# Fetching the last tile of some groups row by row from SyncE's queue in a two-layer graph network

## The chip, the cores and the metric

The kernel runs on one core of a Trainium2 chip. A core has TensorE (PE) for matrix products, VectorE (DVE), ScalarE (ACT), GpSimd (POOL) and SyncE (SP), each with its own queue of instructions, and 16 DMA engines[...]. The metric is device time in microseconds (us), the median of several runs; lower is better.

## The reference

12500 nodes with 64 features, 212500 edges sorted by target node. Each layer gathers a row for the source of every edge, makes a message of it and adds the message to the row of the edge's target. Cut to what matters:

```python
h = jnp.maximum(_layernorm(x, axis=-1), 0.0)
# layer one: 16 relations, each with a 64x64 weight
msg = jnp.zeros(...)
for r in range(16):
    mask = etypes == r
    msg = msg + h[src] * mask[:, None] @ weight[r]
x = x + segment_sum(msg, dst, num_segments=12500)

h = jnp.maximum(_layernorm(x, axis=-1), 0.0)
# layer two
z = relu(concatenate([h[src], h[dst], edge_attr], axis=1) @ W1 + b1)
x = x + segment_sum(z @ W2 + b2, dst, num_segments=12500)
```

All data are float32.

## The kernel before

Edges are taken in order of their targets, 128 at a time: a tile. Four tiles make a group (`G = 4`); there are 1661 tiles with edges (`NTR`) and 416 groups (`NGR`, the last holds one tile). A check in front sends the inputs of this case to `in_order`, which runs `first_layer` and then `second_layer`, each a loop over groups with a few steps lagging behind the group that is being loaded.

**Gathers.** `gather` (line 414) allocates a buffer `rows` of 128 x 4 x 64 values, one of 14, and issues one indirect DMA on GpSimd's queue for every tile of the group (line 419): 128 rows of 256 bytes, from `h_rows` in layer one (the normalised nodes) or from `a_rows` in layer two (the source's part of the first product, W1's upper block applied to the normalised nodes). The row numbers lie in `src_i`, one column per tile. These are GpSimd's only instructions in the two layers.

**Layer one.** For a group, ScalarE makes a one-hot table of relation and target (`relations`, `off_r` and `oh_r`). Two groups later (`L1_PE`) TensorE multiplies each tile's rows with it (`products`, line 577, two matrix products per tile, into `pa`), and five groups later (`L1_ADD`) VectorE adds `pa` into a table of the current nodes. When a block of 256 nodes is complete, `finish` (line 488), spread over the following iterations, applies the relation weights, normalises, and stores `a_rows` and `b_rows` from SyncE's queue. SyncE also loads `part` and `step` (lines 371 to 375) and turns the edge attributes into bfloat16 parts (`attributes`: `attr_a` in, `attr_p` out).

**Layer two.** Per group, SyncE loads `bw` (40 rows of `b_rows` at an address from a register, line 689) and `at9` (the attributes, line 693; `at` in the profile), each with ten buffers, and every fourth group `local_bc` (line 681, three buffers, 480 KB). Every eighth group `windows` (line 436) loads eight addresses into SyncE's registers. ScalarE makes the one-hot `ohT`, TensorE puts target part and attribute part into `pz`. Three groups later (`L2_Z`) VectorE adds the gathered rows: `z = pz + rows` (line 717). Then come the relu (`hid`), the product with a one-hot of the target (`pa`), and the addition into `sums` nine groups later.

**Order.** `V_`, `S_`, `T_` and `Q_` (line 474) keep the instructions of VectorE, ScalarE, TensorE and SyncE in the order in which the program writes them; `Q_` is SyncE. GpSimd's gathers go straight to its queue. A few loads that use `nc.sync` directly may be moved by the scheduler. Buffers are reused when their last reader is done; a DMA of SyncE's queue also waits on the semaphore that the DMA eight places before it used. Layer two's gathers wait until all of `a_rows` is written.

Of the kernel before, what the change touches and what calls it, by code (L numbers as in the profile page):

```python
# [30 lines left out]
F32 = mybir.dt.float32  # L34
BF16 = mybir.dt.bfloat16
I32 = mybir.dt.int32
AF = mybir.ActivationFunctionType
ALU = mybir.AluOpType
# [5 lines left out]
P = 128  # L44
N = 12500
# [29 lines left out]

L1_PE, L1_ADD = (2, 1), (5, 2)
L2_Z, L2_HID, L2_PE, L2_ADD = (3, 1), (4, 1), (6, 1), (9, 1)


def turns(lag):  # L80

    most, least = lag
    of = {}
    for g in range(NGR):
        of.setdefault(g + max(least, min(most, most - (g - (NGR - 40)) // 4)), []).append(g)
    return of
# [40 lines left out]
def gnn_kernel(  # L127
# [161 lines left out]
    def in_order():  # L289
        with ExitStack() as c2:  # L290
# [120 lines left out]
                V_.tensor_scalar(code, d, -1.0, 1.0, op0=ALU.mult, op1=ALU.add)  # L411
                yield

            def gather(table, idx, g):
                t = wk.tile([P, G, D], F32, name="rows", bufs=14)
                tiles = [i for i in range(G) if g * G + i < NTR]
                for i in tiles:
                    k = g * G + i
                    G_.indirect_dma_start(  # L419
                        out=t[:, i, :],  # L420
                        out_offset=None,
                        in_=table,
                        in_offset=bass.IndirectOffsetOnAxis(ap=idx[:, k : k + 1], axis=0),
                    )
                return t, len(tiles)

            def relations(code, k, n):

# [31 lines left out]
            class InOrder:  # L460


                def __init__(self, engine):
                    self.engine = engine
# [102 lines left out]
            def first_layer(psA):  # L567
                local_targets()
                for _ in codes(0, *load_part(0)):
                    pass  # L570
                clear(tables[1][:, :, AHEAD:])
                open_step, beside, coming = iter(()), iter(()), iter(())
                n_of, oh_of, rows_of, pa_of = {}, {}, {}, {}
                of_pe, of_add = turns(L1_PE), turns(L1_ADD)
                chunk = 0

                def products(g, i):
                    for half in range(2):
                        T_.matmul(
                            pa_of[g][half * D : (half + 1) * D, i, :],  # L580
                            lhsT=rows_of[g][:, i, :],
                            rhs=oh_of[g][:, i, half * HW : (half + 1) * HW],
                            start=True,
                            stop=True,
                        )

                def add(a, i):
                    k = a * G + i
                    if i < n_of[a]:
                        ca, ka = divmod(k, NT // NCH)  # L590
                        if k % RG == 0:
                            at.update(enumerate(windows(codes_of[ca][1], ka, SN + AHEAD - WT, V_), k))
                        to = tables[STEP[a] % 2][:, :, bass.ds(at.pop(k), WT)]
                        V_.tensor_tensor(to, to, pa_of[a][:, i, :].rearrange("p (r n) -> p r n", r=RH), op=ALU.add)

                at = {}
                for it in range(NGR + L1_ADD[1]):
                    g = it
                    if g < NGR:
                        c, gc = divmod(g, NGR // NCH)  # L600
                        if gc == NGR // NCH // 4 and c + 1 < NCH:
                            part = load_part(c + 1)
                        if gc == NGR // NCH // 2 and c + 1 < NCH:
                            coming = codes(c + 1, *part)
                        if g % 12 == 6 and chunk < EP // (P // EA) // ACH:
                            for _ in beside:
                                pass
                            beside = attributes(chunk)
                            chunk += 1
                        rows_of[g], n_of[g] = gather(h_rows[:, :], src_i, g)  # L610
                        if n_of[g]:
                            oh_of[g] = relations(codes_of[c][0], gc * G, n_of[g])
                    now, adds = of_pe.get(it, []), of_add.get(it, [])
                    for g in now:
                        if n_of[g]:

                            pa_of[g] = psA.tile([P, G, HW], F32, name="pa", bufs=5)
                    for j in range(max(len(now), len(adds))):
                        for i in range(G):
                            if j < len(now) and i < n_of[now[j]]:  # L620
                                products(now[j], i)
                            if j >= len(adds):
                                continue
                            a = adds[j]
                            add(a, i)
                            for _ in range(1 if a <= FIN[NREG - 1] else 2 if a <= FIN[NFIN - 2] else 3):
                                next(open_step, None)
                            next(coming, None)
                            if i % 2:
                                next(beside, None)  # L630
                        if j < len(adds) and adds[j] in FIN:
                            k = FIN.index(adds[j])
                            for _ in open_step:
                                pass
                            if k + 1 < NFIN:
                                go_on(k)
                            open_step = finish(k, psA)
                for _ in beside:
                    pass
                for _ in open_step:  # L640
                    pass
# [23 lines left out]
            def second_layer(ps):  # L665
# [3 lines left out]
                open_step = iter(())  # L669
                a_of, n_of, oh_of, pz_of, hid_of, pa_of = {}, {}, {}, {}, {}, {}  # L670
                at, at_b = {}, {}
                of_z, of_hid, of_pe, of_add = turns(L2_Z), turns(L2_HID), turns(L2_PE), turns(L2_ADD)
                for it in range(NGR + L2_ADD[1]):

                    g = it
                    if g < NGR:
                        if g % RG == 0:
                            at_b.update(enumerate(windows(first_row, g, PAD_DST, Q_), g))
                        if g % RB == 0:
# [2 lines left out]
                                local_bc,  # L682
                                dst_l[g : g + RB, :].rearrange("g e -> (g e)").unsqueeze(0).to_broadcast([W3, RB * G * P]),
                            )
                        a_of[g], n_of[g] = gather(a_rows[:, :], src_i, g)
                        n = n_of[g]
                        if n:
                            bw = wk.tile([W3, D], BF16, name="bw", bufs=10)
                            Q_.dma_start(
                                bw, b_rows[bass.ds(at_b.pop(g), W), :].rearrange("n (k d) -> k n d", k=3)  # L690
                            )
                            at9 = wk.tile([A9, G * P], BF16, name="at9", bufs=10)
                            Q_.dma_start(
                                at9,
                                attr_p[:, :, g * G * P : (g + 1) * G * P]
                                .rearrange("k i e -> (k i) e")
                                .unsqueeze(0)
                                .to_broadcast([3, 3 * EA, G * P]),
                            )
                            off = wk.tile([W3, G * P], BF16, name="off")  # L700
                            ohT = wk.tile([W3, G * P], BF16, name="ohT", bufs=6)
                            S_.activation(
                                off, local_bc[:, (g % RB) * G * P : (g % RB + 1) * G * P], AF.Abs, bias=neg_w
                            )
                            S_.activation(ohT, off, AF.Relu, bias=1.0, scale=-1.0)
                            if g % 2 == 0:
                                pz = ps.tile([P, 2, G, D], F32, name="pz", bufs=4)
                            pz_of[g] = pz[:, g % 2]
                            for i in range(n):
                                cols = slice(i * P, (i + 1) * P)  # L710
                                T_.matmul(pz_of[g][:, i, :], lhsT=ohT[:, cols], rhs=bw, start=True, stop=False)
                                T_.matmul(pz_of[g][:, i, :], lhsT=at9[:, cols], rhs=w1c_9, start=False, stop=True)
                    for g in of_z.get(it, []):
                        n = n_of[g]
                        if n:
                            hid_of[g] = wk.tile([P, G, D], F32, name="z", bufs=3)
                            V_.tensor_tensor(hid_of[g][:, :n, :], pz_of.pop(g)[:, :n, :], a_of.pop(g)[:, :n, :], op=ALU.add)
                    for g in of_hid.get(it, []):
                        n = n_of[g]
                        if n:  # L720
# [493 lines left out]
```

## Time and profile before

| | us |
|---|---|
| median of three runs (5110.07 to 5111.33) | 5110.31 |
| the profiled execution, its own time | 4236.6 |
| its span, from the first to the last instruction | 4234.8 |
| first gather of layer one starts at | 45.27 |
| first gather of layer two starts at | 2152.24 |

The profiled execution is shorter than the runs that make up the median. All that the profile says is about that one execution. Its TensorE clock was granted in full (1.000).

Some of the stages, as busy time per engine (us from the span's start; the last columns are the share of the 16 DMA engines in use and what they moved):

| stage | length | PE | DVE | ACT | POOL | DMA share | GB/s |
|---|---|---|---|---|---|---|---|
| 1000 to 1500 (layer one) | 500 | 327.1 | 142.2 | 279.2 | 379.0 | 0.20 | 43 |
| 2700 to 3500 (layer two) | 800 | 261.3 | 135.1 | 268.0 | 604.7 | 0.32 | 71 |

How to read the lines further below. A group of instructions is given by source line (L469 is the line of the helper that keeps the order, so many groups share it), engine, operation, what it writes and reads, and its count; then busy time, mean nanoseconds of one, and the idle time of its engine just before, with what ended it. In a list of waits a line is: engine and tile that waited, for what, us in total, times, longest. In a timeline it is: start, duration, instruction, and in brackets the idle time before it. In the answer for one tile, a line is: instruction and count, shortest, median and longest duration in ns, and its first and last start in us. SPq is SyncE's queue; its DMA lines give the issue and not the transfer.

### The profile page before, as it was taken

How to read it: one execution, taken by the hardware profiler on the slowest of the kernel's cores; microseconds unless marked ns; L12 is line 12 of the kernel's file. 1: busy time of each engine (PE TensorE's matmuls, PEld its weight loads, DVE VectorE, ACT ScalarE, POOL GpSimd, SP SyncE). 2: the span in 40 equal slices, each digit the busy share in tenths (PEclk: the TensorE clock that was granted, in tenths of full speed). 3: DMA queues.
4: the chain of work that ended last, by engine and by line, in shares of the span. 5: the costliest groups of instructions: out<-in, count | busy, mean ns of one | idle time of the engine just before them, and what ended most of it. 6: DMA issues, size and time to landing. Idle time of an engine off the chain costs nothing.

```text
span 4234.8 us, 51468 instructions
## 1 busy us (share of the span) xinstructions
PE 2048.8 (48%) x15300; PEld 1509.6 (36%) x15300; DVE 971.8 (23%) x4076; ACT 1884.2 (44%) x3872; POOL 3158.4 (75%) x3342
## 2 busy tenths in 40 slices
PE   1666666666666666666643333333333333333333
PEld 1444434344444444444432222222222223222223
DVE  4222222223222222222211111111111111111111
ACT  6555555555455555554533333333333333333323
POOL 4777777777777777777767777777777777777776
DMA  5212221212122211111133333333333333333332
GB/s 130 43 39 44 43 44 42 44 40 47 39 44 42 44 39 34 32 31 31 32 77 69 74 70 70 73 71 70 69 74 71 69 74 70 70 73 71 70 67 47
DMA packets 289856, 241.32 MB, mean 57 GB/s; under 512 B 177127, under 2 KB 220143, under 8 KB 289463
## 3 DMA queue, kind: packets, MB, share of 16 engines
q0 software_dynamic: 106816, 110.79, 14.5%
q1 hardware_dynamic: 167241, 123.53, 11.0%
q10 hardware_dynamic: 15510, 3.61, 0.4%
q8 instruction: 124, 2.03, 0.2%
q14 instruction: 165, 1.35, 0.1%
HBM read 212.57 MB, written 25.10 MB: 56 GB/s over the span
## 4 chain that ended last, share of the span: by engine, by line
POOL 44%; DMA 29%; issue 23%; PE 5%; ACT 0%; POOLq 0%; DVE 0%; DVEq 0%; ACTq 0%
POOL rows L419 43%; DMA rows<-h_rows,src_i 15%; DMA rows<-a_rows,src_i 13%; PE pT L469 3%; PE pa L469 2%; DMA first_row<-in_first 1%; POOLq L419 0%; PE pab L469 0%; ACT table L469 0%; DVE sums L469 0%; DVE z L469 0%; ACT hid L469 0%; DMA a_rows<-ab 0%; ACT off_r L469 0%; POOLq L1210 0%
## 5 line engine op out<-in xcount | busy, mean ns | idle before, releaser
L419 POOL DMA_INDIRECT rows<-h_rows,src_i x1661 | 1584.7, 954 | 542.1 <-issue 418.8
L419 POOL DMA_INDIRECT rows<-a_rows,src_i x1661 | 1567.2, 944 | 522.3 <-issue 457.7
L469 PE MATMUL pa<-oh_r,rows 128*64 128x96 f32 x6644 | 932.1, 391 | 747.3 <-DMA rows<-h_rows,src_i 656.1
L469 PEld LDWEIGHTS pa<-oh_r,rows 128*64 128x64 f32 x6644 | 502.3, 208 | 1107.4 <-DMA rows<-h_rows,src_i 759.5
L469 PE MATMUL pz<-bw,ohT 120*128 120x64 bf16 x1661 | 231.3, 240 | 1233.6 <-ACT ohT L469 1226.2
L469 ACT ACTIVATE hid<-z 128x256 f32<-128x256 f32 x416 | 173.0, 416 | 1340.4 <-DVE z L469 1321.6
L469 PEld LDWEIGHTS <-ohT 120*128 120x128 bf16 x1661 | 166.0, 125 | 1293.6 <-ACT ohT L469 1286.0
L469 ACT ACTIVATE off_r<-iota_s,code 128x192 bf16<-128x192 f32 x1661 | 616.0, 442 | 4.0 <-DMA w1c<-w1c_p 4.0
L469 DVE TENSOR_TENSOR z<-pz,rows 128x256 f32<-128x256 f32 x416 | 176.6, 424 | 1693.3 <-DMA rows<-a_rows,src_i 1579.0
L469 DVE TENSOR_TENSOR table<-table,pa 128x96 f32 x1661 | 421.3, 254 | 472.2 <-PE pa L469 322.6
L469 PE MATMUL pa<-oh,hid 128*65 128x40 f32 x3322 | 449.4, 309 | 68.2 <-ACT hid L469 54.5
L469 PE MATMUL pT<-wrel,table 128*128 128x64 f32 x1568 | 434.6, 435 | 1.9 <-DVE table L469 1.9
L469 PEld LDWEIGHTS pa<-oh,hid 128*65 128x65 f32 x3322 | 407.8, 229 | 71.9 <-ACT hid L469 57.7
L469 ACT ACTIVATE oh_r<-off_r 128x768 f32<-128x768 bf16 x416 | 350.0, 841 | 183.8 <-PE pa L469 173.0
L469 PEld LDWEIGHTS pT<-wrel,table 128*128 128x128 f32 x1568 | 363.4, 323 | 86.5 <-issue 85.4
L469 ACT ACTIVATE off<-local_bc,neg_w 120x512 bf16<-120x512 bf16 x416 | 294.2, 707 | 35.0 <-DVE sums L469 19.6
L469 ACT COPY table<-zero_c 128x2048 f32<-128x2048 f32 x49 | 93.0, 1897 | 476.0 <-PE pT L469 461.6
L469 ACT ACTIVATE ohT<-off 120x512 bf16<-120x512 bf16 x416 | 261.6, 629 | 13.0
L469 PE MATMUL pz<-w1c,at 72*128 72x64 bf16 x1661 | 232.6, 241 | 7.1 <-DMA at<-attr_p 7.0
L469 PEld LDWEIGHTS <-at 72*128 72x128 bf16 x1661 | 180.6, 128 | 9.0 <-DMA at<-attr_p 8.7
L469 DVE TENSOR_TENSOR oh<-local,iota_p 128x160 f32<-128x160 f32 x416 | 128.8, 310 | 0.0
L469 DVE TENSOR_TENSOR x_sb<-x_sb,pT 128x128 f32<-128x128 f32 (+1 forms) x50 | 14.3, 285 | 430.5 <-PE pT L469 430.5
(101 smaller groups left out, 735.4 us busy)
## 6 DMA issues: line engine op xcount, KB each, us to landing
local_bc<-dst_l SPq DMA_DIRECT2D x104, 480.0 KB
at<-attr_p SPq DMA_DIRECT2D x416, 72.0 KB
rows<-h_rows,src_i POOLq DMA_INDIRECT x1661, 2.5
rows<-a_rows,src_i POOLq DMA_INDIRECT x1661, 2.5
attr_p<-attr_p SPq DMA_DIRECT2D x78, 128.0 KB
attr_a<-in_attr_t SPq DMA_DIRECT2D x26, 256.0 KB
bw<-b_rows SPq DMA_DIRECT2D x416, 15.0 KB
b_rows<-bp SPq DMA_DIRECT2D x48, 96.0 KB
```

The source lines that it names most:

```text
L419: G_.indirect_dma_start(out=t[:, i, :], out_offset=None, in_=table, in_offset=bass.IndirectOffsetOnAxis(ap=idx[:, k : k + 1], axis=0),)
L469: last_ins[self.engine] = getattr(self.engine, name)(*args, **kw)
```

## The change

In every 24th group of layer one (23, 47, ... 407) and every 36th of layer two (35, 71, ... 395), GpSimd gathers three tiles in place of four. The 128 rows of the fourth come into a buffer of their own, `rows_by_hand` (two of them), each row by its own DMA of 256 bytes from SyncE's queue, from an address that is loaded into a register. The row numbers of all these tiles are loaded once per layer into one partition, `by_hand`. The rows are issued ahead in turns: six per group in layer one, four per group in layer two, from the first group of a cycle on, in layer two after the group's `at9`. In layer one the fourth tile's products read the buffer; in layer two VectorE adds it with an instruction of its own.

```diff
+H1, H2 = 24, 36
+def by_hand(g, every):
+    return g % every == every - 1 and (g + 1) * G <= NTR
...
-            def gather(table, idx, g):
+            class ByHand:
+                def __init__(self, table, every):
+                    self.table, self.every, self.rows = table, every, {}
+                    self.groups = [g for g in range(NGR) if by_hand(g, every)]
+                    self.idx = own.tile([1, NGR // H1, P], I32, name="by_hand")
+                    by_group = src.rearrange("(g i p) -> g i p", i=G, p=P)
+                    n = len(self.groups)
+                    Q_.dma_start(
+                        self.idx[:, :n, :], by_group[every - 1 : self.groups[-1] + 1 : every, G - 1, :].unsqueeze(0)
+                    )
+                    self.steps = self.fetch()
+                    self.per_turn = -(-P // (every - 2))
+
+                def fetch(self):
+                    for j, g in enumerate(self.groups):
+                        t = self.rows[g] = wk.tile([P, D], F32, name="rows_by_hand")
+                        for p in range(P):
+                            if p % RG == 0:
+                                at = windows(self.idx[:, j, :], p, N - 1, Q_)
+                            Q_.dma_start(t[p : p + 1, :], self.table[bass.ds(at[p % RG], 1), :])
+                            yield
+
+                def turn(self, g):
+                    if g % self.every < self.every - 2 and g <= self.groups[-1]:
+                        for _ in range(self.per_turn):
+                            if g % self.every * self.per_turn + _ < P:
+                                next(self.steps)
+
+            def gather(table, idx, g, every):
                 t = wk.tile([P, G, D], F32, name="rows", bufs=14)
                 tiles = [i for i in range(G) if g * G + i < NTR]
+                if by_hand(g, every):
+                    tiles = tiles[:-1]
...
-                return t, len(tiles)
+                return t, min(G, max(0, NTR - g * G))
...
+                hand = ByHand(h_rows, H1)
...
                 def products(g, i):
+                    rows = rows_of[g][:, i, :]
+                    if i == G - 1 and by_hand(g, H1):
+                        rows = hand.rows.pop(g)
...
-                            lhsT=rows_of[g][:, i, :],
+                            lhsT=rows,
...
-                        rows_of[g], n_of[g] = gather(h_rows[:, :], src_i, g)
+                        rows_of[g], n_of[g] = gather(h_rows[:, :], src_i, g, H1)
+                        hand.turn(g)
...
+                hand = ByHand(a_rows, H2)
...
-                        a_of[g], n_of[g] = gather(a_rows[:, :], src_i, g)
+                        a_of[g], n_of[g] = gather(a_rows[:, :], src_i, g, H2)
...
+                            hand.turn(g)
...
-                            hid_of[g] = wk.tile([P, G, D], F32, name="z", bufs=3)
-                            V_.tensor_tensor(hid_of[g][:, :n, :], pz_of.pop(g)[:, :n, :], a_of.pop(g)[:, :n, :], op=ALU.add)
+                            z = hid_of[g] = wk.tile([P, G, D], F32, name="z", bufs=3)
+                            a, pz_g = a_of.pop(g), pz_of.pop(g)
+                            if by_hand(g, H2):
+                                n -= 1
+                                V_.tensor_tensor(z[:, n, :], pz_g[:, n, :], hand.rows.pop(g), op=ALU.add)
+                            V_.tensor_tensor(z[:, :n, :], pz_g[:, :n, :], a[:, :n, :], op=ALU.add)
```

## The prediction

> **What bounds the kernel now.** I read the page first (busy shares, the chain that ended last, the costliest groups), then the waits by engine, then POOL's timeline inside each layer and at the seam between them, and last what SyncE does, because the change gives SyncE work.
>
> ```profile
> span 4234.8 us, 51468 instructions
> PE 2048.8 (48%) x15300; PEld 1509.6 (36%) x15300; DVE 971.8 (23%) x4076; ACT 1884.2 (44%) x3872; POOL 3158.4 (75%) x3342
> POOL 44%; DMA 29%; issue 23%; PE 5%; ACT 0%; POOLq 0%; DVE 0%; DVEq 0%; ACTq 0%
> L419 POOL DMA_INDIRECT rows<-h_rows,src_i x1661 | 1584.7, 954 | 542.1 <-issue 418.8
> L419 POOL DMA_INDIRECT rows<-a_rows,src_i x1661 | 1567.2, 944 | 522.3 <-issue 457.7
> ...
> DVE z L469 <- DMA rows<-a_rows,src_i: 1579.0, 379, 7.1
> PEld pa L469 <- DMA rows<-h_rows,src_i: 759.5, 842, 2.9
> ```
>
> POOL is called 75% busy, but its idle time is "issue": it waits for nothing that the profile shows. The chain alternates between POOL's gathers, that issue time and the landing of gathers. The consumers (TensorE in layer one, VectorE's z in layer two) wait for gathered rows, and no other engine reaches half of the span. The timeline shows the rhythm:
>
> ```profile
> 1000.66 0.94 POOL L419 DMA_INDIRECT rows<-h_rows,src_i  x1 [0.30 <-issue]
> 1001.90 0.94 POOL L419 DMA_INDIRECT rows<-h_rows,src_i  x1 [0.30 <-issue]
> 1003.15 0.94 POOL L419 DMA_INDIRECT rows<-h_rows,src_i  x1 [0.30 <-issue]
> ...
> 2134.93 0.94 POOL L419 DMA_INDIRECT rows<-h_rows,src_i  x1 [0.30 <-issue]
> 2152.24 0.94 POOL L419 DMA_INDIRECT rows<-a_rows,src_i  x1 [16.36 <-issue]
> ```
>
> Starts lie 1.25 us apart: 0.94 of work and 0.30 of gap. Layer two shows it cleanly: from 2152.24 to the end of the last gather at about 4225 there are 1661 of them, 1.248 us each. 3322 x 1.248 = 4146 us of the 4234.8. The rest is the front before the first gather (45 us), the seam of 16.4 us between the layers, some slow first gathers, and a tail of under 10 us. Time goes down by 1.248 us for each gather that POOL no longer issues, as long as nobody else becomes late.
>
> Now SyncE, which is to fetch the rows. First the prices of its instructions, then what it waited for from 2300 to 4100 us and, last line, from 100 to 2100 us:
>
> ```profile
> L375 SPq DMA_DIRECT2D step<-in_step_t x8: 224/258/298, 51.3 to 1212.1; - x8
> L469 SPq MOVE bw<-b_rows x416: 29/29/39, 2152.8 to 4172.4; - x139
> L469 SPq DMA_DIRECT2D bw<-b_rows x416: 728/738/1569, 2153.1 to 4173.6; - x139
> L438 SPq TENSOR_LOAD <-first_row x52: 754/774/835, 2151.5 to 4142.8; - x52
> ...
> SPq L469 <- ACT off L469: 604.5, 89, 12.2
> SPq L469 <- PE pa L469: 356.8, 167, 7.5
> SPq L469 <- PE pz L469: 243.2, 125, 5.4
> SPq L469 <- DMA out<-o: 19.8, 3, 9.6
> ...
> SPq L469 <- ACT ab L469: 1222.7, 44, 41.6
> ```
>
> In the 1800 us of layer two SyncE waits 604.5 + 356.8 + 243.2 + 19.8 = 1224 us: it works 32% of the time and has 68% free. In the 2000 us of layer one its waits (the line shown and ten shorter ones) add up to about 1925 us: it works 4%.
>
> [...]Here that issue time is the bound (the DMA engines are 20 to 33% busy in the layers)[...]; the trace has the step row as one 832-byte packet[...].
>
> **The change part by part.**
> Removed: by_hand(g, 24) holds for g = 23, 47, ..., 407, so 17 groups of layer one; by_hand(g, 36) for 35, ..., 395, so 11 of layer two. Each loses its fourth gather. The built order agrees: POOL has 1644 and 1650 gathers in place of 1661 and 1661, and nothing else moves on its queue. 28 x 1.248 = 34.9 us off the bound.
>
> Added on SyncE: 28 x 128 = 3584 one-row DMAs of 256 bytes, a MOVE ahead of each, and one load of eight register values for every eight rows (448). Price of a row: the DMA like the step load, 0.258; MOVE and gap between 0.09 (the gap between bw and at on SyncE's timeline) and 0.25 (between at and the next bw, with MOVE and waits); the load 0.774 / 8 = 0.10. That is 0.45 to 0.61; I take 0.55 us. The upper bound is bw's 0.738 in place of 0.258, since bw also takes its address from a register: 1.09 us. I don't take it, because bw moves 120 short pieces and local_bc, of 120 long ones, is issued in 0.34: the price goes by the shape of the transfer, and a row has one piece.
>
> Does it fit? A cycle of layer one lasts 95 gathers x 1.248 = 118.6 us. SyncE needs 128 x 0.55 = 70 us for rows and 4% (4.7 us) for its own work. A cycle of layer two lasts 143 x 1.248 = 178.5 us; 70 for rows and 32% of 36 old groups of 4.99 us (57.5). Both fit, at 63% and 71%. Within a turn it also fits: 6 rows are 3.3 us in a group of 5.0; 4 rows are 2.2 beside 1.6 us of own work.
>
> Waits: each row's DMA waits on the semaphore of the DMA eight places before it. The packets of one step load show its data 0.9 us after issue[...], against eight rows x 0.55 = 4.4 us, so this wait is met already. Where a local_bc of 480 KB lies eight places back, it lands after about 3.4 us by its packets, also inside. Queued behind SyncE's rows are a_rows, b_rows and attr_p in layer one and local_bc, bw and at in layer two. Layer one's are read much later (attr_p and b_rows in layer two). The last by-hand group is finished before the last blocks, so the a_rows that the seam waits for go out as before and the 16.4 us stay. In layer two SyncE runs up to ten groups ahead, limited by bw's buffers, and loses none of that lead while it is under 100% busy. At the start of layer two it has no lead, but delivers a group in some 3.8 us against POOL's 5.0.
>
> Consumers: rows are complete after turn 21 (layer one) and 31 (layer two), and are used in group 23 two turns later and in group 35 three turns later: four turns and more, 20 us. TensorE's first product with such a tile waits on eight semaphores; VectorE gets 11 more small additions of about 0.2 us. Both have waits of hundreds of microseconds in front of them, which is the cover. If a tile does come late, rows has 14 buffers, so POOL feels nothing until it is some 13 groups (65 us) ahead.
>
> Other effects on POOL: its gathers take 0.94 us both beside SyncE's bursts in layer two and in the quiet layer one, so I charge nothing for the new DMAs; 3584 packets beside 289856 are 1.2%.
>
> Sum against the profiled execution: 4236.6 us (span 4234.8 and 1.8 around it) - 34.9 = 4201.7, -0.82%.
>
> **The median.** The runs shown have 5110.31, 1.2062 times the profiled 4236.6, and nothing in the trace says where the 874 us are. If they lie in every step alike, the saving is 34.9 x 1.2062 = 42.1 us and the time 5068.2. If they are a fixed amount, it is 5075.4. [...]874 / 3322 = 0.26 us per gather is plausible as a slower POOL, while a fixed 874 us has nothing in its favour. I take 5068. SyncE would slow down by the same factor, so the fit above holds.
>
> **Rivals.**
> SyncE becomes the bound: slower. The limit is the row price at which its free time is used up: (118.6 - 4.7) / 128 = 0.89 us in layer one, (178.5 - 57.5) / 128 = 0.95 in layer two. At bw's price of 1.09 layer one needs 139.5 + 4.7 = 144.2 us per cycle, 25.6 too many, x 17 = 435; layer two 197.0, 18.5 too many, x 11 = 204. 4201.7 + 639 = 4841, x 1.2062 = 5839. For it: the register address[...]. Against: the shape argument, and one row's 62 ns of packet time. Chance 0.08.
>
> Half of it is eaten: bursts of rows hold up bw and at so that layer two loses its lead and TensorE and VectorE arrive late at times; half of 42 gives 5089. For it: SyncE's work is bunched by its waits for buffers. Against: 14 buffers. Chance 0.08.
>
> Nothing changes: the gathers' rate is set by their landing and not by POOL's issue, so a missing gather leaves a hole. 5110. Against: a gather lands 2.4 us after its start in the chain, while eight follow each other in 10 us. Chance 0.04. That the gathers are not removed is excluded by the built order.
>
> **Numbers.** All hidden has 0.80, with a range of its own of 5060 to 5078 (both readings of the median). The range 5058 to 5092 adds the half-eaten case. No change means within 0.2% (10 us), about what a measurement of this kernel can tell. Faster 0.87 (all hidden, most of the half-eaten), same 0.05, slower 0.08.
>
> **What would show it.** Right: POOL's gathers 1644 and 1650 at 1.248 us apart, with no idle stretch but the seam, about 16 us; SyncE's row DMA near 0.26 and under 0.6 us per row with its MOVE and load; no long wait of TensorE or VectorE for rows_by_hand. Wrong: rows issued over 0.9 us apart without a wait, TensorE or VectorE waiting for rows_by_hand for tens of microseconds per cycle, POOL idle for buffers of rows, or a gather that grows beyond 0.94 us beside SyncE's rows.

## The result, and the profile after

| | before | changed |
|---|---|---|
| median, us (six runs each, side by side) | 5110.88 (5110.07 to 5113.61) | 5496.69 (5476.89 to 5507.76) |
| ratio to before | | 1.0752, 95% interval 1.0730 to 1.0773 |
| profiled execution, us | 4236.6 | 5507.76 |

The change costs 386 us where the prediction had a gain of 42, and the time lies 405 us above the range's upper end. Executions of this kernel fall into two conditions, a short one in which the kernel before takes about 4237 us and a long one in which it takes 5110 to 5160; a set of runs, with the kernel before run beside the changed one, met one of them or the other as a whole. The profile shown before was of the short condition. The timed runs were all of the long one, and so is the profile of the changed kernel, so the two profiles cannot be subtracted.

The page of the changed kernel, span, busy time and GpSimd's two groups (busy us, mean ns, idle before):

```profile
span 5506.0 us, 62755 instructions
PE 2018.1 (37%) x15300; PEld 1594.1 (29%) x15300; DVE 962.1 (17%) x4087; ACT 1860.5 (34%) x3872; POOL 3133.1 (57%) x3314
...
L461 POOL DMA_INDIRECT rows<-a_rows,src_i x1650 | 1560.6, 946 | 1391.6 <-DVE oh L511 838.9
L461 POOL DMA_INDIRECT rows<-h_rows,src_i x1644 | 1566.0, 953 | 930.1 <-issue 419.6
```

A gather takes 0.95 us as before, and there are 28 fewer of them. But GpSimd now waits: 838.9 us in layer two for VectorE, that is, for `rows` buffers whose readers are late. What they are late for shows in the changed kernel's waits (us in total, times, longest):

```profile
DVE sums L511 <- PE pa L511: 1340.6, 93, 21.9
PEld L511 <- DMA at<-attr_p: 1299.5, 234, 25.1
...
ACT off L511 <- DMA local_bc<-dst_l: 937.9, 82, 61.1
PE pz L511 <- DMA bw<-b_rows: 935.1, 162, 19.5
```

`at`, `local_bc` and `bw` are the three loads that SyncE issues in layer two. TensorE and ScalarE wait for them, VectorE for TensorE, GpSimd for VectorE. SyncE itself hardly waits any more. Its waits from 3000 to 4800 us, in layer two ("remote" is a release that the profile cannot assign):

```profile
SPq L511 <- PE pz L511: 35.7, 69, 1.4
SPq L511 <- PE pa L511: 22.6, 42, 1.0
SPq L511 <- remote: 11.2, 33, 0.7
SPq L511 <- DMA rows_by_hand<-a_rows: 8.0, 17, 1.1
SPq L511 <- PE po L511: 1.1, 2, 0.6
SPq L511 <- DMA at<-attr_p: 0.7, 1, 0.7
```

Together 79 of 1800 us: SyncE works 96% of the time, where work is here, and in all that follows, the time in which it waits for nothing that the profile shows, so time in which it is held up counts as work. In layer two it is the bound, and the rival "SyncE becomes the bound" is what happened.

How slow its instructions are shows in the answer for `rows_by_hand` (shortest, median, longest in ns) and in SyncE's timeline (start, time, rows in the stretch):

```profile
L511 SPq MOVE rows_by_hand<-a_rows x1408: 2/29/1408, 2574.1 to 5387.2; - x176
L511 SPq DMA_DIRECT2D rows_by_hand<-a_rows x1408: 2/225/1397, 2574.1 to 5388.6; - x176
...
3002.07 4.92 SPq L511 DMA_DIRECT2D rows_by_hand<-a_rows  x3
3007.23 0.77 SPq L511 DMA_DIRECT2D bw<-b_rows  x1
3008.10 0.68 SPq L511 DMA_DIRECT2D at<-attr_p  x1
3008.98 1.51 SPq L511 DMA_DIRECT2D rows_by_hand<-a_rows  x4
```

Four rows take 1.51 us at 3009, no more than the prediction's price, and three take 4.92 at 3002. The median DMA is 0.225 us, but some take 1.4, and some are recorded with 2 ns. In the instruction list of that stretch, most register instructions and DMAs last either about 0.70 us or next to nothing, with gaps of about 0.70 before the next: SyncE is held in steps of 0.7 us and then goes on at its old pace.

### The profile page after: what moved, and what is told of

Its sections match the earlier page's. It is cut to its first block, busy times and chain, and to the rows that moved or that the text cites. A ratio compares the mean times of both kernels' runs of the same rounds, so it can differ in the third digit from the quotient of the medians.

```text
span 5506.0 us, 62755 instructions
## 1 busy us (share of the span) xinstructions
PE 2018.1 (37%) x15300; PEld 1594.1 (29%) x15300; DVE 962.1 (17%) x4087; ACT 1860.5 (34%) x3872; POOL 3133.1 (57%) x3314
## 5 line engine op out<-in xcount | busy, mean ns | idle before, releaser
L461 POOL DMA_INDIRECT rows<-a_rows,src_i x1650 | 1560.6, 946 | 1391.6 <-DVE oh L511 838.9
L461 POOL DMA_INDIRECT rows<-h_rows,src_i x1644 | 1566.0, 953 | 930.1 <-issue 419.6
L511 PE MATMUL pa<-oh_r,rows 128*64 128x96 f32 x6576 | 841.2, 368 | 788.4 <-issue 585.4
L511 PEld LDWEIGHTS pa<-oh_r,rows 128*64 128x64 f32 x6576 | 576.4, 213 | 973.2 <-issue 774.3
L511 PE MATMUL pz<-bw,ohT 120*128 120x64 bf16 x1661 | 272.6, 236 | 1536.5 <-DMA bw<-b_rows 935.1
L511 PEld LDWEIGHTS <-at 72*128 72x128 bf16 x1661 | 167.6, 125 | 1621.0 <-DMA at<-attr_p 1299.5
L511 PEld LDWEIGHTS <-ohT 120*128 120x128 bf16 x1661 | 194.8, 132 | 593.4 <-issue 330.0
L511 DVE TENSOR_TENSOR z<-pz,rows 128x256 f32<-128x256 f32 (+1 forms) x416 | 173.4, 417 | 1024.5 <-issue 725.5
L511 DVE TENSOR_TENSOR sums<-sums,pa 65x40 f32 x416 | 76.0, 183 | 1559.7 <-PE pa L511 1340.6
```

The costliest lines, as they stand in the source:

```text
L461: G_.indirect_dma_start(out=t[:, i, :], out_offset=None, in_=table, in_offset=bass.IndirectOffsetOnAxis(ap=idx[:, k : k + 1], axis=0),)
L511: last_ins[self.engine] = getattr(self.engine, name)(*args, **kw)
```

## The experiments

Theory A: the prediction's sum is right in kind, and something else came in with the timed runs. Theory B: SyncE is the bound, because a row costs more on its queue than 0.55 us or because less of its time was free than the profile before said. Each run below has runs of the kernel before beside it; that time says which condition it met. The letters are used anew in later expectations, and each says what its own stand for.

### Is the sum right? (all in the short condition)

The kernel before, unchanged, against itself:

> The kernel before, unchanged, for a second profile. Theory A (GpSimd's gathers bound it, SyncE's queue is what the change overloads): gathers again 1.25 us apart in layer two, SyncE's waits over half of layer two, time 5110 or 4237. Theory B (in the runs of the median something other than GpSimd is the bound, TensorE at half clock or SyncE itself): time 5110, a granted clock near 0.5, and idle stretches of GpSimd that add up to about 870 us.

4237.52 beside 4237.21. It met the short condition, so it says nothing of the runs of the median.

The changed kernel without its row fetches: 28 gathers left out, and those tiles read the rows of the group's third tile.

```diff
-                hand = ByHand(h_rows, H1)
-                        rows = hand.rows.pop(g)
+                        rows = rows_of[g][:, i - 1, :]
-                        hand.turn(g)
```

> The 28 fourth tiles are neither gathered nor fetched: their products and additions read the third tile's rows, so that part of the result is changed. Theory A: the saving of the 28 gathers alone, 28 x 1.25 to 1.5 us = 35 to 42 us, so 5068 to 5075. Theory B: no gain, within 5 us of 5110.

4202.74 beside 4237.21, ratio 0.9918 (0.9902 to 0.9935): 34.5 us less, against 34.9 in the sum.

By hand in layer one only, and in layer two only:

```diff
-H1, H2 = 24, 36
+H1, H2 = 24, None
...
-H1, H2 = 24, 36
+H1, H2 = None, 36
```

> Rows by hand in layer one only. In the changed kernel a cycle of 24 groups takes 142 us in layer one, as long as SyncE needs for its 128 rows. Theory A: slower than 5110 if layer one of the kernel before is faster than that (2090 us in its profile, against 2526): up to +400 us. Theory B (layer one is bound elsewhere in the runs of the median): within 50 us of 5110.

> Rows by hand in layer two only. Theory A: SyncE's 128 rows and 72 larger DMAs take 255 us a cycle against 180, so layer two is longer by 11 x 75 = 800 us than in the profile of before, less where the runs of the median are slower than that profile; 5400 to 5500. Theory B: about 5110 plus what bw and at come late, below 5300.

4214.39 (0.9945, interval 0.9928 to 0.9962) and 4223.80 (0.9967, 0.9954 to 0.9979): 22.8 and 13.4 us less, for 17 and 11 gathers. Both expectations had counted on the long condition.

The changed kernel, unchanged:

> The changed kernel, unchanged, on the chip on which the kernel before takes 4237 us and each layer's half of the change saves 22.8 and 13.4 us. Theory C (the two halves add, and the loss on record comes from a condition of those runs in which SyncE's instructions are held up in steps of 0.7 us): 4237 - 36 = about 4201. Theory D (the two halves together overload SyncE's queue in any run): about 5500, with SyncE's stretches of 0.7 us in the trace.

4199.92 beside 4237.03, ratio 0.9911 (0.9898 to 0.9925): 37.1 us faster. GpSimd's two groups on the page and the answer for `rows_by_hand` in this run:

```profile
L461 POOL DMA_INDIRECT rows<-h_rows,src_i x1644 | 1566.8, 953 | 537.6 <-issue 415.8
L461 POOL DMA_INDIRECT rows<-a_rows,src_i x1650 | 1556.9, 944 | 519.1 <-issue 445.3
...
L511 SPq MOVE rows_by_hand<-a_rows x1408: 29/29/38, 2134.4 to 4065.5; - x176
L511 SPq DMA_DIRECT2D rows_by_hand<-a_rows x1408: 224/225/414, 2134.5 to 4065.6; - x176
```

GpSimd has its old gaps and no more, and no instruction of a row is held. The same program is 0.9% faster in one condition and 7.5% slower in the other.

### How much more would SyncE bear? (short condition)

All gathers kept and read, the rows fetched as well and read by nobody:

```diff
-                if by_hand(g, every):
-                    tiles = tiles[:-1]
...
-                        rows = hand.rows.pop(g)
+                        hand.rows.pop(g)
```

Layer two's additions read the gathered rows in the same way.

> All 3322 gathers stay, and SyncE fetches the 3584 rows as well, unread. Where SyncE has room for them (rows at 0.54 us each, as in the trace of the changed kernel at 4200 us): no change, 4237 within 8 us. Where a row costs over 0.9 us, as in the changed kernel's profile at 5506 us (142 us for 128 rows in layer one): slower by several hundred us, without any gather missing.

4233.95 beside 4236.86, 0.9993 (0.9984 to 1.0002): SyncE's extra work alone costs nothing here.

Each row fetched twice, and three times, the others into unread buffers; one line of two:

```diff
                             Q_.dma_start(t[p : p + 1, :], self.table[bass.ds(at[p % RG], 1), :])
+                            Q_.dma_start(u[p : p + 1, :], self.table[bass.ds(at[p % RG], 1), :])
```

> Each row is fetched twice, the second time into a buffer that nobody reads, so a row costs SyncE 0.54 + 0.41 = 0.95 us. Theory C (the sum of the prediction with the row's price as its only unknown): layer one needs 128 x 0.95 + 4.7 = 126 us a cycle against 118.6, layer two 122 + 57.5 = 179 against 178.5: 4200 + 17 x 7.7 + 11 x 0.6 = about 4340. Theory D' (SyncE's price does not matter, the loss on record has another cause): 4200.

> Each row three times, two of them unread: 1.36 us a row. Theory C: layer one 174 + 4.7 against 118.6, layer two 174 + 57.5 against 178.5: 4200 + 17 x 60 + 11 x 53 = about 5800, and the picture of the changed kernel's profile at 5506: GpSimd idle for buffers, TensorE waiting for at and bw. Theory D': 4200.

4575.1 (ratio 1.0798, 1.0780 to 1.0816) and 6058.2 (1.4298, 1.4275 to 1.4322). Both cost more than expected. With two, SyncE takes 125 us to issue a cycle's 128 rows in layer one, where the prediction's cycle lasts 118.6 us, and about 189 us in layer two, where it lasts 178.5. The same waits as in the changed kernel appear, here with two DMAs a row:

```profile
ACT off L513 <- DMA local_bc<-dst_l: 1254.5, 98, 28.9
DVE sums L513 <- PE pa L513: 1151.2, 111, 14.4
PEld L513 <- DMA at<-attr_p: 1007.8, 308, 6.3
```

So a full SyncE gives the signature of the result in the short condition too, in which no row's DMA of the changed kernel is under 224 ns. The time from one DMA to the next, read from the instruction list, is 0.41 us for the register arithmetic, MOVE and DMA, and a row has an eighth of about 1 us for the load besides: 0.54.

The rows taken more often, `H1, H2 = 18, 26`, 23 and 15 tiles in place of 17 and 11:

> Every 18th group of layer one and 26th of layer two, 23 and 15 tiles by hand in place of 17 and 11. Theory C at 0.54 us a row: 69 + 3.6 of 88.6 us a cycle, 69 + 41.5 of 128.5: it fits, and 38 x 1.248 = 47 us are saved, 4190. If SyncE is nearer to its limit than that: above 4200.

4189.97 beside 4236.86, 0.9892 (0.9875 to 0.9908), as expected. It is the best version seen, in the short condition only; it was not tried in the long one.

As the kernel with unread rows, but from rows 0 to 127 of the table each time, so that load and register instructions fall away:

```diff
-                            if p % RG == 0:
-                                at = windows(self.idx[:, j, :], p, N - 1, Q_)
-                            Q_.dma_start(t[p : p + 1, :], self.table[bass.ds(at[p % RG], 1), :])
+                            Q_.dma_start(t[p : p + 1, :], self.table[p : p + 1, :])
```

> All gathers are kept and read; SyncE issues the same 3584 one-row DMAs into the unread buffers, but from fixed rows (row p for lane p), so that the register loads and the two register instructions ahead of each row are left out: one instruction a row in place of 3.1. Beside before at 5110 to 5160, theory B1 (what is held is each instruction of SyncE's queue) expects a third of the loss of the kernel with fetched and unread rows, a ratio of about 1.02 to 1.04 against 1.0857; theory B2 (it is the DMAs, their descriptors or their packets) expects the same ratio, 1.07 to 1.09. If before takes 4237, both expect 4234 and nothing is told apart.

It met the short condition: 4235.64 beside 4237.69, and told nothing apart. The same went for these two, which repeat the kernels with one layer by hand:

> By hand in layer one only, as before when it took 4214 beside 4237. If before takes 5110 to 5160 here: the profiles of the changed kernel and of before in this condition put the start of layer two at about the same place and all of the difference into layer two, so theory B expects no loss, a ratio of 0.995 to 1.005; a theory that charges every row alike expects 17 of 28 of the loss, a ratio of about 1.045.

> By hand in layer two only, 4224 beside 4237 before. If before takes 5110 to 5160 here: theory B expects the whole loss of the changed kernel, a ratio of 1.07 to 1.08; charging every row alike gives 11 of 28 of it, a ratio of about 1.03.

4213.0 and 4224.56 beside 4237.69. Which layer loses in the long condition was therefore not tried alone.

Three DMAs a row from fixed rows:

> All gathers kept and read; every one-row DMA from a fixed row is issued three times, into three unread buffers: three DMAs a row and no register instruction, so about as many instructions on SyncE (10752) as the kernel whose rows were fetched through registers and unread (11,200). In the condition in which before takes 5110 to 5160: if each instruction of SyncE's queue is held alike, whatever its kind, the ratio is 1.07 to 1.10 (1.0857 there); if it is the register instructions and loads that cost, and a DMA of fixed address is cheap, it stays at 1.002 to 1.02. In the other condition three DMAs at 0.25 us are 0.77 us a row, under the 0.89 that the prediction names as the limit, so 4234 to 4245 is expected and it tells only that 10752 DMAs of one row are not the cost there.

4611.24 beside 4236.28, 1.0891 (1.0873 to 1.0910): it met the short condition, and the expectation of 4234 to 4245 was wrong. Such a DMA takes 0.25 us and starts 0.295 after the one before it, so three are 0.885 us, not 0.77. SyncE's waits name a second cost:

```profile
SPq L511 <- DMA at<-attr_p: 255.8, 352, 1.3
```

SyncE's DMAs take eight semaphores in turn (in the changed kernel's profile 92% take the one that the DMA eight places before took), and 4767 of the 4780 there wait on their own before they start. At 0.295 us apart eight places are 2.4 us; the last packet of an `at` ends 3.2 us after its issue (median of 96 in the profile before), and the waits for `at` here are up to 1.3 us long. All of the loss is in layer two, where `at` is loaded: the last gather of layer one starts at 2133.0 us, and at 2134.9 in the profile before.

### What is held in the long condition

The changed kernel once more:

> The changed kernel once more, in another job, to see whether the condition of the runs on record (before 5110, changed 5497) comes back. If it does: 5450 to 5510 beside 5110, with SyncE's stretches of 0.7 us. If not: 4200 beside 4237, within 3 us of the run before.

5509.19 beside 5109.44, 1.0761 (1.0728 to 1.0793): the result came back. The condition does not go with the chip: two chips met both (the kernel before took 4236.86 and 5159.97 on one, 4237.69 and 5111.28 on the other).

The kernel before, for a profile, and with it the kernel that keeps all gathers and fetches rows that nobody reads:

> The kernel before, unchanged, for a profile in the condition in which its runs take 5110 us and not 4237 (neither the page before the prediction nor the first repeat had one). If this run takes about 5110: theory A, everything is stretched evenly by 1.206, then GpSimd's gathers start 1.505 us apart throughout and its row of the groups shows a longer mean or gap; theory B, SyncE's instructions are held in steps of 0.7 us and it is SyncE that has no time left, then the gathers keep 1.25 us, layer one stays near 2100 us, and GpSimd idles in layer two for buffers by about 870 us in sum, since layer two is where SyncE had 32% of its own work. If this run takes 4237 the condition did not come and nothing is told apart.

> All 3322 gathers are issued by GpSimd and read; the 3584 rows are fetched by SyncE as well but nobody reads them. Undisturbed it took 4233.95. If the runs of before beside it take 5110: theory B (SyncE is the bound in this condition, so its rows are the cost and the gathers removed are worth nothing) expects 5450 to 5560, as the changed kernel; theory A (an even stretch, and the changed kernel is late because its consumers wait for the rows) expects about 5110. If before takes 4237 it expects 4234 again.

Before took 5160.29 beside 5162.02, the other 5599.41, 1.0857 (1.0839 to 1.0875), 39 us above what theory B expected. With no gather removed, the rows alone bring the loss. The page of the kernel before in this condition:

```profile
span 5152.0 us, 51468 instructions
...
L419 POOL DMA_INDIRECT rows<-a_rows,src_i x1661 | 1567.0, 943 | 1062.9 <-issue 516.3
L419 POOL DMA_INDIRECT rows<-h_rows,src_i x1661 | 1576.7, 949 | 892.0 <-issue 420.0
```

A gather takes 943 to 949 ns, as in the short condition: nothing is stretched evenly. GpSimd's idle time before its gathers is 1062.9 + 892.0 - 542.1 - 522.3 = 890 us longer than in the profile before, most of the 917 us between the spans. GpSimd is no longer the bound, in either layer. Theory B named layer two and SyncE alone for that, and was too narrow: layer one is longer too (its last gather starts at 2476.9, and at 2134.9 in the short profile), and TensorE is held as well. TensorE's weight loads from 3065 to 3080 us, with the idle time ahead of each in brackets:

```profile
3065.80 0.18 PEld L469 LDWEIGHTS pa<-oh,hid 128*65 128x65 f32 x1 [1.92 <-issue]
3067.23 0.19 PEld L469 LDWEIGHTS pa<-oh,hid 128*65 128x65 f32 x1 [1.24 <-issue]
3069.65 0.18 PEld L469 LDWEIGHTS pa<-oh,hid 128*65 128x65 f32 x1 [2.23 <-issue]
...
3079.49 0.10 PEld L469 LDWEIGHTS <-at 72*128 72x128 bf16 x1 [0.59 <-issue]
3079.51 0.11 PEld L469 LDWEIGHTS <-ohT 120*128 120x128 bf16 x1
3079.55 0.13 PEld L469 LDWEIGHTS <-at 72*128 72x128 bf16 x1
```

After a burst of several dozen, TensorE's weight loads come one in 0.7 to 2.8 us for some 18 us with nothing they wait for ("issue"), and then at their old pace until 3086.8 us, where the next such stretch begins, 25 us or four groups after this one. SyncE's waits from 3000 to 4800 us of the kernel before:

```profile
SPq L469 <- PE pz L469: 285.7, 84, 8.6
SPq L469 <- remote: 131.1, 24, 10.5
SPq L469 <- PE pa L469: 86.2, 67, 7.8
```

These and six shorter lines give 536 of 1800 us, 30% free, where the profile before had 68%. Divided by the groups gathered meanwhile (1155 gathers, 289 groups), SyncE works 4.38 us a group, against 1.60 in the short condition: (1700 - 1154) us over 340.5 groups in the short repeat of before.

The kernel with fixed rows again, and then two fixed DMAs a row:

> As the kernel with fixed rows before it, which met an undisturbed run (4235.64 beside 4237.69). If before takes 5110 to 5160 here: theory B1 (each instruction of SyncE is held) expects a ratio of 1.02 to 1.04; theory B2 (the DMAs themselves) 1.07 to 1.09, the 1.0857 of the kernel with fetched, unread rows. If before takes 4237, again nothing.

> All gathers kept and read; two DMAs a row from fixed rows into two unread buffers: two instructions a row, 2 x 0.295 = 0.59 us of SyncE's undisturbed time, about what a row through registers takes (0.54). If before takes 5110 to 5160 here: a charge per instruction of SyncE expects a ratio half way between one instruction a row (1.0021) and 3.1 (1.0857), 1.03 to 1.05; a charge for the register instructions alone expects 1.002 to 1.01; a charge by SyncE's undisturbed time per row expects 1.08 or more. If before takes 4237: 0.59 us a row is below the limit of 0.89 in layer one and the 0.88 that was already over it in layer two, so 4234 to 4245.

Both met the long condition. The kernels beside one another there; SyncE's work is (1800 us less its waits) divided by the groups gathered from 3000 to 4800 us. The ratios compare runs side by side; the two columns in us come from sets in which before took 5110 (the second and the last row) or 5160 us (the others), which is 1%:

| SyncE's instructions for a row | ratio to before | us a group | SyncE's work a group |
|---|---|---|---|
| none (before) | 1 | 6.23 | 4.38 |
| 1: DMA from a fixed row | 1.0021 (1.0013 to 1.0030) | 6.15 | 5.83 |
| 2: two such DMAs | 1.0368 (1.0350 to 1.0387) | 6.63 | 6.14 |
| 3.1: load, register arithmetic, MOVE, DMA; unread | 1.0857 (1.0839 to 1.0875) | 7.11 | 6.79 |
| 3.1: the changed kernel | 1.0761 (1.0728 to 1.0793) | 7.07 | 6.74 |

The kernels with one and with two fixed DMAs a row issue as many DMAs of 256 bytes as the one with unread rows, or twice as many, and cost less. A charge by DMAs is excluded, and so is a charge by SyncE's undisturbed time per row, which is 0.59 us for two DMAs and 0.54 through registers. The cost rises with the number of SyncE's instructions. One a row cost less than either theory expected (1.02 to 1.04, or 1.07 to 1.09): it fills SyncE's free time almost exactly, and only further ones come on top, two a row inside the 1.03 to 1.05 of a charge per instruction. That the kind of instruction plays no part is not shown, because three fixed DMAs a row met the short condition. Nor is it shown what the removed gathers are worth here: the last two rows differ by 1%, and so do the sets that they come from.

## Why the prediction was wrong

**What held, in the condition that its profile showed.** The 28 gathers are worth 34.5 us alone (34.9 in the sum), and 37.1 with the rows. The split by layers is as the count says. A row costs SyncE 0.54 us (0.55). SyncE's waits in the changed kernel leave 575 of 1500 us free in layer one and 481 of 1700 in layer two, 38% and 28%, where the prediction had 37% and 29%. (It counted a MOVE ahead of each row's DMA; the kernel has a second register instruction there, FUSED_REGOPS, 37 ns. That is 3.1 instructions a row and not 2.1, at the time that it had forecast.)

**The step that failed** is the sentence "SyncE would slow down by the same factor, so the fit above holds", and with it the reading of the 1.2062 between median and profiled execution as an even stretch, which was the author's estimate and shown by no trace. A gather of layer two takes 944 ns in the profile before and 943 in the long run of before, which rules an even stretch out here. GpSimd's pace did not change; SyncE's own work in layer two went from 1.60 to 4.38 us a group, by 2.7 and not by 1.2, and that used up the room for the rows.

The row's price was not the error. In the profile of the changed kernel shown above SyncE works 6.72 us a group, (6.72 - 4.38) / (128 / 36) = 0.66 us for a row, which is 0.55 times 1.206; as held time counts as work, that this is so close is luck. With the measured own work the prediction's fit for layer two, as an estimate, reads: 36 x 4.38 + 128 x 0.66 = 242 us for a cycle of 36 groups that lasts 36 x 6.23 = 224 in before. It doesn't fit. As rows are issued in only 32 of the 36 turns, the cycle becomes 32 x (4.38 + 4 x 0.66) + 4 x 6.23 = 249.6, 25 too many, and for 11 cycles 278 us. Layer two lasted 5506.0 - 2570.4 = 2935.6 us against 5152.0 - 2537.8 = 2614.2: 321 more. What makes up the other 43 is not shown; the two profiles come from sets that differ by 1%. Layer one adds 33 us (2570.4 - 2537.8), though SyncE is full there too: from 500 to 2000 us it waits 41 us in the changed kernel and 802 in the long run of before (1434 in the short repeat). The load that is waited for there is `attr_a` (ScalarE's `attr_p`, 253 us in that stretch), and the 33 us say that this held up little else.

**The rivals.** "SyncE becomes the bound" named the mechanism and, under "what would show it", the signs that came: GpSimd idle for buffers of `rows`, rows issued over 0.9 us apart. Its price was wrong twice: a row has not `bw`'s 1.09 us, and SyncE's own work was not 4% and 32%, but 47% and 70% of the stretches compared here; the two errors gave 5839 for 5497. Its limit of 0.89 us a row in layer one held in the short condition: at 0.885 (three fixed DMAs) that layer lost nothing. The limit of 0.95 in layer two was too generous: at 0.885 the kernel lost 8.9%, all of it there. The wait for `at` eight places back is part of that, 255.8 us; that SyncE's work comes in bursts is the likely rest, and not tested.

**What the profile before could have told.** Not the 4.38 us. But a profiled execution 874 us below runs that agree within 1.3 us says that the profile is of something else, and then the headroom read from it, on the one queue that the change loads, has no support in either direction. A chance of 0.08 for the rival whose limit was computed from that headroom was too low.

## What to carry to other kernels

Compare the profiled execution with the median first; where they differ by far more than the runs differ among themselves, a fit into another queue's free time cannot be read from that profile, nor scaled. When work moves to a queue that others depend on, count the instructions it adds there, not only their time: here, in the long condition, one a row was almost free and three cost 8%. A queue with loads that others wait for costs nothing until it is full and then much (here nothing with one fetch a row and 8% with two, in the short condition), so double the moved work once on purpose to see how far off the edge is.

## What the runs showed of the hardware

**Held instructions.** In the long condition TensorE and SyncE are held in steps of 0.70 us. Of SyncE's 8002 register instructions (MOVE and FUSED_REGOPS) in the changed kernel's profile 1184 last 0.68 to 0.72 us and 2501 under 0.02; all 834 in the profile before last 0.03 to 0.05. Of SyncE's DMA records 24% last under 20 ns in the changed kernel's profile, and none is under 0.22 us in the profile before. Of TensorE's `pT` weight loads that follow another one directly and without a wait of their own, 1133 in the profile before, none starts over 0.22 us after the one ahead of it (0.21 at the median); in the changed kernel's profile 83 of 1143 start over 0.5 us after it, 58 of them within 0.06 us of 0.7, 1.4 or 2.1 us.

The two engines are held together: in the changed kernel's profile 1029 instructions of TensorE start over 0.6 us after its last one and within 0.35 us of an end of a SyncE step (a register instruction or a gap of 0.64 to 0.76 us), and 673 of them start in the 50 ns after it, where chance would put one in fourteen; of ScalarE's 40 of 613 do, of GpSimd's 84 of 1405. (An example from the long run of before is 3067.23 in the list above, where SyncE's DMA starts at 3067.20.) This speaks for one thing that holds both. The medians of GpSimd's gathers (0.944 us in the profile before, 0.947 in the changed kernel's), of ScalarE's `off_r` (0.439 and 0.441) and of VectorE's `table` (0.255 in both) stay, and so, within 5%, does that of the instruction fetches' packets (0.53 and 0.52). No instruction is fetched in the changed kernel's profile from 3018.4 to 3046.0 us, which takes in a held stretch of SyncE (3025.7 to 3037.0). What holds the two engines is open, and no run shows what brings the long condition on.

**The granted clock was no cause.** It was 0.526 in the changed kernel's profile and 0.524 in the long run of before, but also 0.53 in the short condition with three fetches a row. The median product of layer one (`pa`) takes 367 ns at 0.526 and 368 at 1.0, and the kernel before took the same time in short executions at 0.747 and at 1.0 (4237.45 and 4237.0 us).

**Prices.** A one-row DMA from a fixed address takes 0.25 us and follows the last after 0.295; from an address in a register it takes 0.225 and follows after 0.41, with its two register instructions.
